# Layer 0's attention: turning the negated maxima on VectorE in squares of 32, and sixteen transfers a round into q's stacks

## The chip, the cores and the metric

The program runs on one core of one Trainium2 chip, as one launch. The time is the device time of one execution in microseconds (us). Three executions of the kernel before took 2251.18, 2256.95 and 2261.61 us; the median is 2256.95. A profile is one more execution, recorded by the hardware profiler.

A core has five engines that work side by side and wait for each other through semaphores: TensorE (PE in the profile; its weight loads are PEld), VectorE (DVE), ScalarE (ACT), GpSimd (POOL) and SyncE (SP), which here issues nearly all DMA transfers. Each engine takes its instructions in the order of the program.

## The reference, cut to what matters

The whole is a decoder of four layers on x of shape 4 x 512 x 128: each layer has a self-attention, a cross-attention and a feed-forward part. Only layer 0's self-attention is touched. It has 16 heads of 8 channels, a causal mask and a linear bias in the distance (ALiBi), and a temperature:

```python
att = jnp.einsum('bqhd,bkhd->bhqk', q, k) * scale
att = att / temperature
bias = slopes[:, None, None] * rel[None, :, :]
bias = jnp.where(causal[None, :, :], bias, -jnp.inf)
att = att + bias[None, :, :, :]
w = jax.nn.softmax(att, axis=-1)
y = jnp.einsum('bhqk,bkhd->bqhd', w, v).reshape(Bc, Tc, Cc)
return y @ W_proj + b_proj
```

The softmax is computed as exp(att - maximum over the keys), divided by its sum.

## The kernel before

**Stages.** `build` runs the parts one after another and weaves a main stream with a side chain: after each step of the main stream, a step of the side chain is emitted. In the first stage the main stream is `rounds` of `l0_attn`; the side chains are layer norms, the context of layer 0's cross-attention, that cross-attention for batches 0 and 1, and the router of the first feed-forward part. A planner then settles each engine's instruction order from the dependences and its own estimates of durations; within an engine that order is fixed when the program runs. The feed-forward part of layer 0 follows.

**Stacks.** For each group of four heads there is a stack `qs[g]` and a stack `ks[g]`: a tile of 99 rows, 4 heads and 512 tokens in bfloat16. A product of the two stacks sums over rows. Rows 0 to 71 hold q and k, each number split into three bfloat16 parts, rows 72 to 80 the position bias, and rows 96 to 98 of q's stack the three parts of the negated maximum of every query, against ones in k's stack. So the scores to find the maxima use 81 rows (line 1136), and the scores for `exp` use all 99 (line 1181): the maximum is then already subtracted in the product. That second product has keys on the partitions and queries along the free axis, so the negated maxima must lie along a row, while the reduction that makes them leaves queries on the partitions. They must be turned.

**Rounds.** An item is one batch with one group of four heads; there are 16 items. In round r the kernel works at once on the item `now` (scores and maxima, `score_units`, 11 units), on `prev` (the item before: its maxima are turned and its first 5 units of `exp` start) and on `old` (its last 6 units of `exp`, then `values`). Divisions and the closing product of a batch come for the item before that. A round has 11 steps; in each step one score unit and one unit of `exp` are emitted. The `exp` units of `old` fill steps 0 to 5, those of `prev` steps 6 to 10.

**The maxima.** At step 0 `shift` cuts the 128 x 16 negated maxima m (16 = 4 blocks of 128 tokens x 4 heads) into three bfloat16 parts with four small VectorE operations (lines 1155 to 1158; subtractions are recorded under the helper `tt`, line 436) and leaves them in `d3`. At step 2 `shift_rows` turns them: four TensorE transposes, one for each block of 128 tokens, into one PSUM bank of 12 x 512 (line 1165), one ScalarE copy to `d_rows` (line 1167), and four transfers from SyncE, one for each head, each of 3 rows of 512 tokens, into rows 96 to 98 of `qs[g]` (line 1169). At step 7 `load` issues six transfers (lines 1125 and 1126) that fill the stacks of the item two rounds on. In rounds 1, 5 and 9 (counted by the item whose maxima are turned), the projections of the next batch are computed and stored with four transfers (lines 1109 and 1111). All of these go through SyncE's one queue, in order.

Of the kernel before, what the change touches and what calls it, by code (L numbers as in the profile page):

```python
# [14 lines left out]
BF16 = mybir.dt.bfloat16  # L15
# [3 lines left out]
ALU = mybir.AluOpType  # L19
# [3 lines left out]
P = 128  # L23
B, S, D = 4, 512, 128
NT = B * S // P
TB = S // P
# [265 lines left out]
class Net:  # L292
# [745 lines left out]
    def l0_attn(self, pool, W, Wo):  # L1038
# [3 lines left out]
        nc, tc = self.nc, self.tc  # L1042
        one = lambda shape, name, dt=F32: pool.tile(shape, dt, name=name, bufs=1)
        K1, K2 = 81, 99
        qs = [one([K2, 4, S], f"qs{g}", BF16) for g in range(4)]
# [18 lines left out]
        rows = one([48, 16], "own_rows")  # L1064
# [8 lines left out]
        def biases():  # L1073
            ps = self.mm((1, D))
            self.dot(ps, *[(Wo["bv"][:, g : g + 1], Wo["wp"][:, g * D : g * D + D]) for g in range(4)])
            br = one([1, D], "br")
            self.tt(br, ps, Wo["bp"], ALU.add)
            wp0 = one([P, D], "wp0")
            nc.vector.tensor_copy(wp0, Wo["wp"][:, :D])
            nc.sync.dma_start(wp0[8:9, :], br)  # L1080
            wp.extend([wp0] + [Wo["wp"][:, g * D : g * D + D] for g in range(1, 4)])

        items = [(b, g) for b in range(B) for g in range(4)]
        made, ys, stacks = {}, {}, {}

        def project(b):

            xb = self.tokens(b)
            pq, pk = self.mm(), self.mm()
            self.dot(pq, (W["wq"], xb))  # L1090
            self.dot(pk, (W["wk"], xb))
            q, k = (pool.tile([P, S], F32, tag=n, name=n, bufs=1) for n in "qk")
            nc.vector.tensor_scalar(q, pq, W["bq"], sc, ALU.add, ALU.mult)
            nc.scalar.activation(k, pk, AF.Identity, bias=W["bk"])
            yield
            q3, k5 = pool.tile([P, 3, S], BF16, tag="q3", name="q3"), pool.tile([P, 5, S], BF16, tag="k5", name="k5")
            for a, out in ((q, q3), (k, k5)):
                nc.scalar.copy(out[:, 0], a)
                self.tt(a, a, out[:, 0], ALU.subtract)
            yield  # L1100
            for a, out in ((q, q3), (k, k5)):
                nc.scalar.copy(out[:, 1], a)
                self.tt(out[:, 2], a, out[:, 1], ALU.subtract)
            yield
            nc.gpsimd.tensor_copy(k5[:, 3:5], k5[:, 0:2])
            qd = self.away.tile([16, 24, S], BF16, name=f"q_parts{b}")
            kd = [self.away.tile([16, 24, S], BF16, name=f"k_parts{b}_{c}") for c in range(3)]
            flat = lambda d: d.rearrange("h (d p) t -> (h d) (p t)", p=3)
            nc.sync.dma_start(flat(qd), q3.rearrange("r p t -> r (p t)"))
            for c in range(3):  # L1110
                nc.sync.dma_start(flat(kd[c]), k5[:, c : c + 3].rearrange("r p t -> r (p t)"))
            stacks[b] = qd, kd
            yield
            ps = self.mm((P, TB, 16, 8))
            for j in range(TB):
                self.dot(ps[:, j].rearrange("p h d -> p (h d)"), (self.tile_of(TB * b + j), W["wv"]))
            nc.scalar.copy(vs[b % 2][:, :, :, :8], ps)
            yield

        def load(b, g):  # L1120

            qd, kd = stacks[b]
            for c in range(3):
                r = slice(24 * c, 24 * c + 24)
                nc.sync.dma_start(qs[g][r], qd[4 * g : 4 * g + 4].rearrange("h r t -> r h t"))
                nc.sync.dma_start(ks[g][r], kd[c][4 * g : 4 * g + 4].rearrange("h r t -> r h t"))

        def score_units(b, g):

            m = made[b, g, "m"] = pool.tile([P, TB, 4], F32, tag="m", name="m", bufs=2)  # L1130

            def unit(i, h0, per):
                n = (i + 1) * P
                ps = self.mm((P, per, n))
                for h in range(per):
                    nc.tensor.matmul(  # L1136
                        ps[:, h], lhsT=qs[g][:K1, h0 + h, i * P : n], rhs=ks[g][:K1, h0 + h, :n], start=h == 0, stop=False
                    )
                nc.tensor.matmul(  # L1139
                    ps[:, :, i * P :], lhsT=self.identb, rhs=self.causal.unsqueeze(1).to_broadcast([P, per, P]),  # L1140
                    start=False, stop=True,
                )
                nc.vector.tensor_reduce(m[:, i, h0 : h0 + per], ps, AX.X, ALU.max, negate=True)  # L1143

            return [
                lambda i=i, h0=h0, per=per: unit(i, h0, per)
                for i, per in ((3, 1), (2, 1), (1, 2), (0, 4)) for h0 in range(0, 4, per)
            ]

        def shift(b, g):  # L1150

            m = made.pop((b, g, "m"))
            d3 = made[b, g, "d"] = pool.tile([P, TB, 4, 3], BF16, tag="d3", name="d3")
            rest = pool.tile([P, TB, 4], F32, tag="d_rest", name="d_rest")
            nc.vector.tensor_copy(d3[..., 0], m)
            self.tt(rest, m, d3[..., 0], ALU.subtract)
            nc.vector.tensor_copy(d3[..., 1], rest)
            self.tt(d3[..., 2], rest, d3[..., 1], ALU.subtract)

        def shift_rows(b, g):  # L1160

            d3 = made.pop((b, g, "d"))
            t = self.bank("mm", [12, S], BF16)
            for i in range(TB):
                nc.tensor.transpose(t[:, i * P : i * P + P], d3[:, i].rearrange("q h p -> q (h p)"), self.identb)
            rows = pool.tile([12, S], BF16, tag="d_rows", name="d_rows", bufs=2)
            nc.scalar.copy(rows, t)
            for h in range(4):
                nc.sync.dma_start(qs[g][96:99, h, :], rows[3 * h : 3 * h + 3, :])

        def exp_units(b, g):

# [50 lines left out]
        def divide(b):  # L1223
            y = ys[b]
            dT = self.turned3(inv.pop(b), pool)
            for g in range(4):
                c = self.mm()
                self.dot(c, (pick[:, 4 * g : 4 * g + 4].rearrange("r h i -> r (h i)"), dT))
                self.tt(y[:, g, :], y[:, g, :], c, ALU.mult)
# [8 lines left out]
        def rounds(first, last):  # L1238
            n = len(items)
            item = lambda i: items[i] if 0 <= i < n else None  # L1240
            if first == 0:
                yield from project(0)
                load(0, 0)
                biases()
                load(0, 1)
                yield
            for r in range(first, last):
                now, prev, old, done = (item(r - i) for i in range(4))
                a = score_units(*now) if now else []
                if prev:  # L1250
                    made["units", prev] = exp_units(*prev)
                late = made.pop(("units", old))[5:] if old else []
                early = made["units", prev][:5] if prev else []
                ahead = project(now[0] + 1) if now and now[1] == 1 and now[0] + 1 < B else iter(())
                for i in range(11):
                    if i == 0 and prev:
                        shift(*prev)
                    if i == 2 and prev:
                        shift_rows(*prev)
                    if i < len(a):  # L1260
                        a[i]()
                    e = late[i : i + 1] if i < 6 else early[i - 6 : i - 5]
                    for unit in e:
                        unit()
                    yield
                    if i == 1 and done and done[1] == 3:
                        divide(done[0])
                        yield
                    if i == 4 and done and done[1] == 3:
                        close(done[0])  # L1270
                        yield
                    if i == 7 and old:
                        values(*old)
                        yield
                    if i == 9 and old and old[1] == 3:
                        sums(old[0])
                        yield
                    if i in (1, 3, 5, 8, 10):
                        next(ahead, None)
                    if i == 7 and item(r + 2):  # L1280
                        load(*item(r + 2))
# [1103 lines left out]
```

## Time and profile before

| what | value |
|---|---|
| time, median of 3 runs | 2256.95 us |
| the profiled execution's own time | 2272.79 us |
| its span, first to last instruction | 2271.0 us |
| mean granted TensorE clock | 0.957 |
| PE busy over the span | 2109.5 us, 93% |
| DVE busy over the span | 1608.1 us, 71% |
| ACT busy over the span | 995.4 us, 44% |
| attention stage, 40 to 253 us: PE busy | 196.05 us |
| the same: DVE busy | 153.62 us |
| the same: ACT busy | 127.92 us |
| d_rows transfers | 64 of 3.0 KB, first issue at 43.3 us, last at 253.1 us |

The span is divided among engines by busy time, and a chain of work is followed back from the last instruction. A busy share says how much an engine did, not what the end waited for; for that one reads, in the stage concerned, what each engine waited for and who released it. A row of the timeline has the start, the length, the engine, the line, the operation with output and inputs, the count, and in brackets the idle time before it and its releaser. A row of a line's list has shortest, median and longest duration in ns. A row of windows has the stretch, its length, the busy time of PE, PEld, DVE, ACT and POOL (instructions in brackets), then the granted TensorE clock as a share of full speed, the busy share of the DMA engines and GB/s. Lengths of matmuls are modelled and overlap.

### The profile page before, as it was taken

The page shows a single profiled execution, that of the slowest core. Times are in us where ns is not written, and L with a number is a line of the kernel's source. Part 1 is how long each engine was busy: PE and PEld are TensorE (multiplying, and loading weights), DVE is VectorE, ACT ScalarE, POOL GpSimd, SP SyncE. Part 2 cuts the span into 40 slices and gives each one's busy share as a digit, 9 for nine tenths or more (in the row PEclk, how much of TensorE's full clock was granted, in tenths as well). Part 3 has the DMA queues.
Part 4 walks back from the last instruction along what each step waited for, and adds up shares of the span by engine and source line. Part 5 has one row for each costly group of instructions (what it writes and reads, how often), then busy time and mean ns, then how long its engine had stood idle before and what let it go on. Part 6 is the DMA issues. An engine that isn't in the chain of part 4 may idle for free.

```text
span 2271.0 us, 28138 instructions
## 1 busy us (share of the span) xinstructions
PE 2109.5 (93%) x8946; PEld 1121.5 (49%) x8946; DVE 1608.1 (71%) x4059; ACT 995.4 (44%) x2042; POOL 554.8 (24%) x695
## 2 busy tenths in 40 slices
PE   6999899999999998999999999999999996697778
PEld 3566556544545553444444544444444443564463
DVE  6667576666675769787977797867777765886525
ACT  4556446444325452444434543443343434364421
POOL 1000001000000001433323343333333322336541
PEclk7989999999999999999999999999999998898869
DMA  6321134254453344334334444444443442200022
GB/s 167 99 65 44 45 111 123 62 137 112 112 143 84 105 101 107 75 100 110 110 83 105 114 120 114 124 111 107 114 114 101 111 129 46 94 1 6 20 54 76
DMA packets 88947, 213.26 MB, mean 94 GB/s; under 512 B 21874, under 2 KB 40626, under 8 KB 88542
## 3 DMA queue, kind: packets, MB, share of 16 engines
q1 hardware_dynamic: 85230, 207.52, 34.9%
q0 software_dynamic: 3568, 3.93, 0.6%
q8 instruction: 71, 1.16, 0.2%
q14 instruction: 78, 0.64, 0.1%
HBM read 182.33 MB, written 23.53 MB: 91 GB/s over the span
## 4 chain that ended last, share of the span: by engine, by line
PE 72%; DVE 15%; issue 5%; ACT 3%; POOL 2%; DMA 2%; SPq 1%; another core or an unknown queue 0%; POOLq 0%; DVEq 0%; ACTq 0%
PE mm L425 19%; PE f L425 13%; PE mm L1854 8%; PE s L425 8%; PE acc L1013 6%; PE mm L1826 4%; PE mm L1801 4%; DVE h L436 2%; PE mm L1136 1%; PE mm L1203 1%; PE mm L1181 1%; DVE at_m L1883 1%; DVE m L1143 1%; DVE gvx L436 1%; PE s L515 1%
## 5 line engine op out<-in xcount | busy, mean ns | idle before, releaser
L1762 POOL TENSOR_TENSOR gvx<-gvx 128x512 f32<-128x512 f32 (+1 forms) x256 | 260.3, 1017 | 549.3 <-DVE gvx L436 488.3
L425 PE MATMUL f<-xT,w_l_ffn 128*128 128x512 f32 (+1 forms) x768 | 369.3, 603 | 1.2 <-ACT h L1005 0.7
L1885 ACT ACTIVATE at_e<-mm,at_m 128x512 f32<-128x512 f32 x256 | 173.0, 685 | 293.1 <-DVE at_m L1883 274.3
L425 PE MATMUL mm<-w_l_ffn_qkv,xT 128*128 128x512 f32 x512 | 266.3, 604 | 4.2 <-ACT at_e L1885 1.7
L1854 PE MATMUL mm<-og,w_l_ffn_o 128*128 128x512 f32 x512 | 265.8, 603 | 3.2 <-DVE og L436 3.2
L436 DVE TENSOR_TENSOR h<-h,f 128x512 f32<-128x512 f32 (+1 forms) x192 | 131.1, 684 | 139.9 <-PE f L425 105.3
L1005 ACT ACTIVATE h<-f 128x512 f32<-128x512 f32 x189 | 112.3, 596 | 251.0 <-PE f L425 214.2
L425 PEld LDWEIGHTS f<-xT,w_l_ffn 128*128 128x128 f32 (+1 forms) x768 | 140.2, 192 | 151.0 <-issue 123.6
L1013 PE MATMUL acc<-h,w_l_ffn 128*128 128x512 f32 x378 | 194.8, 600 | 3.5 <-DVE h L436 2.9
L436 DVE TENSOR_TENSOR gvx<-mm,gv 128x512 f32<-128x512 f32 x256 | 174.5, 683 | 20.8 <-PE mm L425 17.1
L436 DVE TENSOR_TENSOR og<-mm,c 128x512 f32<-128x512 f32 x256 | 176.2, 690 | 18.3 <-PE mm L1854 16.0
L1802 ACT COPY eT<-mm 128x512 f32<-128x512 f32 x256 | 137.6, 596 | 83.4 <-PE mm L1801 83.2
L1883 DVE TENSOR_REDUCE at_m<-mm 128x1 f32<-128x512 f32 x256 | 161.1, 681 | 11.7 <-PE mm L425 10.3
L1801 PEld LDWEIGHTS mm<-ident,at_e 128*128 128x128 f32 x1024 | 120.2, 142 | 68.4 <-issue 47.7
L1854 PEld LDWEIGHTS mm<-og,w_l_ffn_o 128*128 128x128 f32 x512 | 91.7, 191 | 114.4 <-issue 90.3
L1801 PE MATMUL mm<-ident,at_e 128*128 128x128 f32 x1024 | 135.1, 274 | 5.3 <-ACT at_e L1885 5.3
L425 PEld LDWEIGHTS mm<-w_l_ffn_qkv,xT 128*128 128x128 f32 x512 | 87.3, 190 | 95.2 <-issue 59.0
L425 PE MATMUL mm<-roped 64*128 64x512 f32 x512 | 131.3, 622 | 1.7 <-DVE roped L436 1.0
L1143 DVE TENSOR_REDUCE m<-mm 128x1 f32<-128x512 f32 (+3 forms) x176 | 104.8, 635 | 32.6 <-PE mm L1139 31.7
L1826 PE MATMUL mm<-eT,v 128*64 128x512 f32 x512 | 118.7, 599 | 0.0
L1013 PEld LDWEIGHTS acc<-h,w_l_ffn 128*128 128x128 f32 x378 | 71.2, 192 | 93.1 <-issue 67.3
L436 DVE TENSOR_TENSOR h<-h,c 128x512 f32<-128x512 f32 x160 | 111.5, 703 | 4.1 <-DMA c<-l_ffn_w 1.3
(453 smaller groups left out, 3529.4 us busy)
## 6 DMA issues: line engine op xcount, KB each, us to landing
c<-gates SPq DMA_DIRECT2D x256, 256.0 KB
c<-l_ffn_w SPq DMA_DIRECT2D x96, 384.0 KB
w_l_ffn<-in_l_ffn SPq DMA_DIRECT2D x26, 576.0 KB
w_l_ffn_qkv<-in_l_ffn_qkv SPq DMA_DIRECT2D x16, 640.0 KB
w_l_ffn_o<-in_l_ffn_o SPq DMA_DIRECT2D x16, 512.0 KB
rot<-qk SPq DMA_DIRECT2D x128, 64.0 KB
d<-inverted SPq DMA_DIRECT2D x64, 128.0 KB
k_parts<-k SPq DMA_DIRECT2D x12, 384.0 KB
```

The lines of the kernel that those rows point to most:

```text
L425: self.nc.tensor.matmul(out, lhsT=lhsT, rhs=rhs, start=i == 0, stop=i == len(pairs) - 1)
L436: self.nc.vector.tensor_tensor(out, a, b, op)
L1005: nc.scalar.activation(h, pg, AF.Silu)
L1013: nc.tensor.matmul(acc["t"], lhsT=W["d" + u], rhs=h, start=i == 0, stop=i == n - 1)
L1143: nc.vector.tensor_reduce(m[:, i, h0 : h0 + per], ps, AX.X, ALU.max, negate=True)
L1762: nc.gpsimd.tensor_tensor(x[:, :, :m], x[:, :, :m], x[:, :, m : 2 * m], ALU.add)
L1801: nc.tensor.transpose(p[:, j, :], es[i][hl][:, j * P : j * P + P], self.ident)
L1802: nc.scalar.copy(eT[hl][:, :, i * P : i * P + P], p)
L1826: nc.tensor.matmul(po[64 * hl : 64 * hl + 64, :], lhsT=m["v"][:, j, hl, :], rhs=eT[hl][:, j, :], start=j == 0, stop=j == TB - 1,)
L1854: nc.tensor.matmul(acc, lhsT=W["o"][:, (e - 1) * D : e * D], rhs=hs.pop(e - 1), start=e == 1, stop=e == E)
L1883: nc.vector.tensor_reduce(m, s, AX.X, ALU.max, negate=True)
L1885: nc.scalar.activation(e[:, :n], s, AF.Exp, bias=m, accum_out=den)
```

## The change

`d3` becomes one tile that stays, 128 x 4 x 32 in bfloat16, cleared once on GpSimd. Of each 32 columns the first 12 hold the parts (4 heads x 3 parts). `shift` writes them there with the same four small operations, and then turns the whole tile on VectorE with one instruction, which turns each square of 32 partitions x 32 columns in itself. After it, partition 32k + 3h + p holds, for block j and the 32 columns of that square, part p of head h for the tokens 128j + 32k to 128j + 32k + 31. The four groups of 32 partitions therefore hold different tokens, and each head's row is put together by four transfers: 4 groups x 4 heads make sixteen a round, each of 3 rows and 4 runs of 32 tokens (64 bytes). They are issued group by group, with the heads inside. `shift_rows`, with its transposes, its PSUM bank and its ScalarE copy, is gone, and so is its call at step 2.

```diff
+        d3 = one([P, TB, 32], "d3", BF16)
+        nc.gpsimd.memset(d3, 0.0)
+
         def shift(b, g):
 
             m = made.pop((b, g, "m"))
-            d3 = made[b, g, "d"] = pool.tile([P, TB, 4, 3], BF16, tag="d3", name="d3")
+            parts = d3[:, :, :12].rearrange("q j (h p) -> q j h p", p=3)
             rest = pool.tile([P, TB, 4], F32, tag="d_rest", name="d_rest")
-            nc.vector.tensor_copy(d3[..., 0], m)
-            self.tt(rest, m, d3[..., 0], ALU.subtract)
-            nc.vector.tensor_copy(d3[..., 1], rest)
-            self.tt(d3[..., 2], rest, d3[..., 1], ALU.subtract)
-
-        def shift_rows(b, g):
-
-            d3 = made.pop((b, g, "d"))
-            t = self.bank("mm", [12, S], BF16)
-            for i in range(TB):
-                nc.tensor.transpose(t[:, i * P : i * P + P], d3[:, i].rearrange("q h p -> q (h p)"), self.identb)
-            rows = pool.tile([12, S], BF16, tag="d_rows", name="d_rows", bufs=2)
-            nc.scalar.copy(rows, t)
-            for h in range(4):
-                nc.sync.dma_start(qs[g][96:99, h, :], rows[3 * h : 3 * h + 3, :])
+            nc.vector.tensor_copy(parts[..., 0], m)
+            self.tt(rest, m, parts[..., 0], ALU.subtract)
+            nc.vector.tensor_copy(parts[..., 1], rest)
+            self.tt(parts[..., 2], rest, parts[..., 1], ALU.subtract)
+            rows = pool.tile([P, TB, 32], BF16, tag="d_rows", name="d_rows", bufs=2)
+            nc.vector.transpose(rows.rearrange("q j r -> q (j r)"), d3.rearrange("q j r -> q (j r)"))
+            for k in range(4):
+                for h in range(4):
+                    nc.sync.dma_start(
+                        qs[g][96:99, h, :].rearrange("p (j k r) -> k p j r", k=4, r=32)[k],
+                        rows[32 * k + 3 * h : 32 * k + 3 * h + 3],
+                    )
...
                     if i == 0 and prev:
                         shift(*prev)
-                    if i == 2 and prev:
-                        shift_rows(*prev)
```

## The prediction

> **What bounds the kernel now.** I read the page first (busy shares, chain), then the attention stage alone, 40 to 253 us.
>
> ```profile
> span 2271.0 us, 28138 instructions
> PE 2109.5 (93%) x8946; PEld 1121.5 (49%) x8946; DVE 1608.1 (71%) x4059; ACT 995.4 (44%) x2042; POOL 554.8 (24%) x695
> PE 72%; DVE 15%; issue 5%; ACT 3%; POOL 2%; DMA 2%; SPq 1%; another core or an unknown queue 0%; POOLq 0%; DVEq 0%; ACTq 0%
> ```
>
> TensorE is the bound nearly everywhere, and runs in order: a wait at its head that nothing fills lengthens the run. In this stage it is busy 196.05 of 213 us, so it has about 17 us to give. The whole change lies here, in a loop: the maxima of round r-1 are cut into three parts, turned, and carried by DMA into rows 96 to 98 of q's stack, which the first `exp` unit of round r (line 1181, 99 rows) reads. Round 3 in the timeline of all engines (start us, length us):
>
> ```profile
> 63.50 0.68 DVE L1143 TENSOR_REDUCE m<-mm 128x1 f32<-128x512 f32 x1
> 64.52 0.18 DVE L436 TENSOR_TENSOR d<-d_rest,d 128x16 bf16<-128x16 f32 x1
> 64.75 0.39 PE L1165 MATMUL mm<-identb,d 128*12 128x128 bf16 x4 [1.35 <-DVE d L436]
> 65.22 0.57 ACT L1167 COPY d_rows<-mm 12x512 bf16<-12x512 bf16 x1 [1.29 <-PE mm L1165]
> 65.83 2.78 SPq L1169 DMA_DIRECT2D qs<-d_rows  x4
> 67.64 0.38 PE L1181 MATMUL mm<-qs,ks 99*128 99x512 bf16 x1
> 68.33 0.10 PEld L1181 LDWEIGHTS <-ks 99*128 99x128 bf16 x1 [0.31 <-DMA qs<-d_rows]
> 74.08 0.17 DVE L1155 CAST d<-m 128x16 bf16<-128x16 f32 x1
> ```
>
> The reader is to see that there is no slack left. The first transfer is issued at 65.83 and head 0's matmul starts at 67.64: 1.8 us from issue to use. Head 1's transfer starts about 0.7 us later and head 1's matmul, at 68.33, is released by it. The list of line 1169 gives what one such issue holds SyncE for, and one 512-byte transfer in sixteen pieces of 32 bytes (line 1080) shows that pieces do not raise it:
>
> ```profile
> L1169 SPq DMA_DIRECT2D qs<-d_rows x64: 639/642/782, 43.3 to 253.1; - x64
> L1080 SPq DMA_DIRECT2D wp<-br x1: 638/638/638, 25.3 to 25.3; - x1
> ```
>
> Four take 2.78 us: 0.64 plus a gap of 0.07, 0.71 us from one to the next.
>
> **What goes.** Sixteen rounds each lose four PE transposes (0.39 us), one ScalarE copy (0.57) and TensorE's wait for d (1.35 in round 3). The path from the last small VectorE operation to SyncE, 64.70 to 65.83, 1.1 us, goes with them.
>
> **What comes.** One VectorE turn of 128x128 bf16. The trace has no such operation: from the 0.17 us of a 128x16 cast to the 0.68 us of a 128x512 reduction; the Trainium skill ("VectorE: DVE Perf Modes", The three transpose paths) states 311 ns, between the two. I take 0.3. The memset on POOL comes once, before the rounds, off the path. Then sixteen issues on SyncE in place of four. Head 0 reads all 512 tokens, and the transfers go block by block with the heads inside, so head 0 is complete with the thirteenth: 12 x 0.71 = 8.5 us after the first issue. Landing of the thirteenth: 1.8 us as now (3 rows either way; four runs of 64 bytes each instead of one of 1024; from 1.5 to 2.3).
>
> **What is moved.** In the changed program's instruction order the turn does not follow the four small operations at once. In eight of the rounds (3, 4, 7, 8, 11, 12, 13, 15) score reductions of the running round stand between them: cast, reduction, subtraction, reduction, cast, reduction, subtraction, reduction, turn. Reductions run 0.57 apart in this stage (0.6 with the switch), the small ones 0.2: 4 x 0.6 + 3 x 0.2 + 0.3 + 0.1 = 3.4 us from the first cast to SyncE. Before, round 3 needed 65.83 - 63.43 = 2.4.
>
> So from the first cast to head 0's matmul: 3.4 + 8.5 + 1.8 = 13.7 us. Before, from the timeline, in those eight rounds: 4.21, 4.22, 4.80, 5.17, 4.85, 5.17, 4.26, 4.63, in all 37.3. Increase: 8 x 13.7 - 37.3 = 72.3 us. The others, by how many operations stand before the turn:
> - Rounds 1 and 16 (none): 1.1 + 8.5 + 1.8 = 11.4, before 5.23 and 4.57: +6.2 and +6.8.
> - Round 2 (one reduction): 12.0, before 5.96: +6.0.
> - Rounds 5 and 9 (a reduction and q's scaling, 0.8): 12.8, before 5.28 and 5.69: +7.5 and +7.1.
> - Rounds 6, 10 and 14: TensorE has the closing products of a batch in that stretch, 11.1, 16.1 and 13.2 us; the transfers need about 12.5: +1.5, 0, 0. These products are the cover.
>
> Sum +107 us. From head 0's matmul to the next round's cast is TensorE's own stream, 6.4 us in plain rounds (67.64 to 74.08), and passes on unchanged: heads 1 to 3 arrive 0.71 apart, no faster than TensorE takes them. The next round waits for this stretch, so nothing absorbs the delay; the planner only moves work of the side chain (layer norm, cross-attention of batches 0 and 1, the router) ahead of head 0 in rounds 7, 8, 11, 12 and 13. That takes some 2 us from elsewhere and fills, but does not shorten, the wait: +105.
>
> What queues behind the sixteen on SyncE: six loads of q's and k's stacks for two rounds on (0.41 each), and in three rounds q's and k's stores. 16 x 0.71 + 6 x 0.41 = 13.8 us a round against a new round of 13.7 + 6.4 = 20 us: SyncE doesn't become a bound of its own, and the loads have a round to spare.
>
> **The clock.** TensorE would now stand some 8 to 10 us in thirteen rounds (it reaches head 0 about 4 us after the cast). What idling does to it shows after round 1 and at the stage's end (windows; the third number from the right is the granted clock):
>
> ```profile
> 43.00:46.00 3.00, 1.45 (x12) 0.69 (x10) 3.00 (x6) 2.62 (x6) 0.00 (x0) 1.00 0.01 2
> 46.00:50.00 4.00, 2.94 (x17) 1.58 (x17) 4.00 (x7) 2.13 (x4) 1.04 (x1) 0.62 0.52 125
> 50.00:54.00 4.00, 4.00 (x19) 2.87 (x17) 2.43 (x8) 1.62 (x4) 0.00 (x0) 0.53 1.01 356
> ...
> 265.00:268.00 3.00, 0.76 (x6) 0.52 (x6) 1.40 (x5) 0.57 (x1) 0.00 (x0) 0.57 0.58 152
> 268.00:272.00 4.00, 3.95 (x13) 2.54 (x13) 2.48 (x4) 1.29 (x2) 0.00 (x0) 0.50 1.04 249
> 272.00:275.00 3.00, 3.00 (x16) 3.00 (x16) 0.00 (x0) 0.00 (x0) 0.00 (x0) 0.50 1.01 223
> ```
>
> After some 3 us of idling at 265 the clock stays at half for about 7.5 us of full work. The Trainium skill ("TensorE: Matmul & The Clock Gate", Part 1) says the same in a rule that speaks against this change: an idle window of about 3.4 us halves the clock, a busy one restores it, and the windows run free. By row and rule half speed lasts 3.4 to 7.5 us after each long wait and costs half of that, 1.7 to 3.7 us; I take 2.8. Thirteen rounds give 36 us, less about 8 for half-clock spells that the stage already has (the one at 46 to 54, which the new wait swallows, and part of the others): +28. Without the gate the sum would stay at +105.
>
> A second rule says the opposite of my main term: "DMA: Bandwidth & Descriptors", Issuing engines are not separate DMA queues, calls the issuing time usually small beside the transfer. Here the row decides: 0.64 us of issue against 1.8 us to use, for 3 KB in all. Were it small, say 0.05, head 0 would wait 3.4 + 0.6 + 1.8 = 5.8 us and the eight rounds would lose only 8 x 5.8 - 37.3 = 9 us together.
>
> **Sum.** 105 + 28 = +133 us. The profiled execution took 2272.79 us (span 2271.0); with 133 it is 2406. The median of the runs shown, 2256.95, lies 16 below that execution; the same difference gives 2390.
>
> **Rivals.**
> 1. Issue-bound, clock free: the wait as above, but what follows it is held by VectorE (reductions 0.57 apart) and ScalarE (`exp` 0.56) so that a halved TensorE costs little. Against: the values matmuls, 2.3 us a round, are TensorE alone. +105: 2362.
> 2. Pieces cost: twelve runs of 64 bytes raise the issue to about 1.0 us or slow three DMA engines. Against: line 1080's row. 12 x 1.0 + 5.2 = 17.2 us, 3.5 more in thirteen rounds, with the clock +180: 2437.
> 3. Issues are cheaper: q's loads, also 3-D but from DRAM, take 0.37. Then 12 x 0.41 = 4.9, the wait 10.1, 3.6 less in thirteen rounds: +60 to +85, about 2330.
> 4. Faster: the issue overlaps fully and head 0 is released by the first-landed transfers. It decides where the spacing falls below some 0.05 us and VectorE, no longer held up by TensorE's stop at the transposes, turns a reduction or two sooner, so that the path is under the 4.7 us of before; then the PE transposes, their waits (up to 1.35 us in six rounds) and the copies are gain, 5 to 15 us: 2245. Against: 0.71 is measured for the same source, destination and row count.
> 5. The change does nothing: the wait is filled by the side chain. Against: that chain has about 10 us in all, against 105.
>
> **How the numbers follow.** Forecast 0.70; rivals 1 to 5: 0.11, 0.09, 0.06, 0.03, 0.01. The forecast's own spread (landing 1.5 to 2.3, half clock 1.7 to 3.7) is about 2370 to 2420. Range 2345 to 2440: it takes in rival 1 and the lower half of rival 2, and leaves out rivals 3 to 5 and the upper half of 2, some 15 in 100. A measurement of this kernel tells about 0.5% (11 us) from no change: faster 0.03, same 0.01, slower 0.96.
>
> **What would show it.** In the profile after: line 1167's issue near 640 ns, sixteen in some 11.3 us per round; TensorE's weight loads before the 99-row matmuls waiting for d_rows for 80 to 120 us in all (7.2 before); 13 to 14 us from the first cast to head 0 in rounds 3 and 4; granted clock about half in the stage's windows after each wait; the stage's end some 130 us later and all after it alike. Wrong would be: an issue far from 0.64, a release before the thirteenth transfer, or a clock that stays full.

## The result, and the profile after

The changed kernel takes 2390.79 us (median; 2388.53 to 2392.19) against 2259.28 us (2251.18 to 2264.16) for the kernel before: 1.0579 times as long, 95% interval 1.0551 to 1.0606, or 131.5 us more. The forecast was 2390, range 2345 to 2440.

The page's head (span, busy time of each engine) of the kernel after:

```profile
span 2389.7 us, 28258 instructions
PE 2128.1 (89%) x8882; PEld 1120.6 (47%) x8882; DVE 1615.5 (68%) x4075; ACT 989.8 (41%) x2026; POOL 554.8 (23%) x696
```

TensorE has 64 instructions fewer (the transposes), ScalarE 16 fewer (the copies), VectorE 16 more (the turns), POOL one more (the memset). TensorE's share falls from 93% to 89%: the added time is time in which it stands. Where that is, three stretches of the run show (length of the stretch, busy PE, PEld, DVE, ACT, POOL, granted clock, DMA share, GB/s). Before, from the end of the attention stage on:

```profile
253.00:2173.00 1920.00, 1811.22 (x6929) 938.55 (x6928) 1386.66 (x3429) 832.16 (x1721) 504.26 (x630) 0.97 0.38 98
2173.00:2271.00 98.00, 78.69 (x288) 45.01 (x286) 43.08 (x83) 21.58 (x47) 31.24 (x32) 0.85 0.14 46
```

After, the attention stage, and then the same two stretches:

```profile
40.00:391.00 351.00, 221.11 (x1596) 130.75 (x1593) 161.46 (x452) 122.32 (x232) 11.40 (x12) 0.75 0.14 40
391.00:2311.10 1920.10, 1813.27 (x6927) 938.75 (x6927) 1386.49 (x3429) 831.92 (x1720) 503.81 (x630) 0.97 0.38 98
2311.10:2389.70 78.60, 69.88 (x288) 38.10 (x286) 42.66 (x83) 21.72 (x47) 31.19 (x32) 0.98 0.18 58
```

The middle, 1920 us, is the same to 0.1 us. The attention stage is 138 us longer (head 0 of round 16 starts at 390.56 instead of 252.79). The last stretch is 19 us *shorter* after, with the same instructions at a clock of 0.98 instead of 0.85. That is a property of the one execution that was profiled before, which the prediction found 16 us above the median: in the traces of all nine other kernels of this document, from their last 288 matmuls on, this stretch takes 78.9 to 79.4 us, in the trace of before 98.5. So the spans differ by 118.7, the medians by 131.5, and the stage by 138. The reader should take the stage from the traces and the total from the medians. The 6.5 us between these two lie within the spread of the kernel before (2249.37 to 2267.90 us in 27 executions) and are not explained further.

Round 3 in the timeline of the kernel after (start, length, engine, line, operation, and in brackets the idle time before it and its releaser), to set beside round 3 of before:

```profile
79.88 0.18 DVE L1159 CAST d<-m 128x16 bf16<-128x16 f32 x1
...
82.46 0.31 DVE L1164 STREAM_TRANSPOSE d_rows<-d 128x128 bf16<-128x128 bf16 x1
82.80 12.01 SPq L1167 DMA_DIRECT2D qs<-d_rows  x16
93.69 0.58 PE L1182 MATMUL mm<-qs,ks 99*128 99x512 bf16 x1 [11.28 <-DMA qs<-d_rows]
...
102.74 0.18 DVE L1159 CAST d<-m 128x16 bf16<-128x16 f32 x1
```

From the cast to the first issue 2.9 us, sixteen issues in 12.0 us (0.75 us apart), and head 0's matmul 10.9 us after the first issue. Twelve spacings are 9.0 us, so the thirteenth transfer leaves at 91.8 and is used 1.9 us later. TensorE stood for 11.28 us just before. The list of line 1167 (shortest, median, longest ns) has the new transfers; the turn, line 1164, is listed with 295, 306 and 314 ns, sixteen times:

```profile
L1167 SPq DMA_DIRECT2D qs<-d_rows x256: 702/703/886, 41.7 to 391.1; - x128
```

TensorE's waits in the attention stage (total, times, longest; matmuls, then weight loads), after and then before:

```profile
PE mm L1182 <- DMA qs<-d_rows: 112.1, 13, 11.5
PEld L1182 <- DMA qs<-d_rows: 75.9, 19, 11.8
```

```profile
PE mm L1181 <- DMA qs<-d_rows: 1.8, 2, 1.5
PEld L1181 <- DMA qs<-d_rows: 7.2, 15, 1.8
```

And the granted clock (third number from the right) over round 3, after and then before:

```profile
82.00:86.00 4.00, 0.41 (x3) 0.10 (x1) 1.67 (x5) 0.76 (x2) 0.00 (x0) 0.99 0.10 25
86.00:90.00 4.00, 0.00 (x0) 0.00 (x0) 0.00 (x0) 0.00 (x0) 0.00 (x0) 0.50 0.01 1
94.00:98.00 4.00, 4.00 (x22) 1.30 (x24) 0.56 (x1) 1.19 (x2) 0.00 (x0) 0.50 0.38 104
98.00:102.00 4.00, 4.00 (x40) 2.24 (x33) 1.76 (x3) 1.96 (x4) 0.00 (x0) 0.80 0.58 167
```

```profile
60.00:74.00 14.00, 12.62 (x127) 7.38 (x119) 9.41 (x19) 9.84 (x18) 0.00 (x0) 1.00 0.44 116
```

From 86 to 90 no engine computes, and the DMA engines are idle too (0.01): only SyncE issues. When TensorE starts again it is fully busy, but at half clock for the first 4 us and more.

To compare kernels, each round is split at two events that all of them have: the first cast of the maxima, and head 0's 99-row matmul. The sums, in us, over the stage (cast to head 0: 16 rounds; head 0 to the next cast: 15), with the time for which TensorE's clock was at half between 36 and 420 us (read in windows of 1 us):

| kernel | cast to head 0 | head 0 to next cast | sum | half clock | median, us | ratio (95%) |
|---|---|---|---|---|---|---|
| before | 104.4 | 108.4 | 212.8 | 54 | 2256.96 to 2259.92 | 1 |
| after | 216.4 | 133.8 | 350.2 | 192 | 2390.79 | 1.0579 (1.0551 to 1.0606) |
| heads_outer | 132.9 | 179.6 | 312.5 | 148 | 2371.42 | 1.0473 (1.0422 to 1.0525) |
| pe_turn_16 | 214.1 | 133.4 | 347.5 | 167 | 2392.78 | 1.0575 (1.0532 to 1.0619) |
| clock_kept | 217.1 | 114.0 | 331.1 | 47 | 2378.73 | 1.0529 (1.0482 to 1.0576) |
| two_queues | 167.1 | 130.0 | 297.1 | 145 | 2347.89 | 1.0386 (1.0352 to 1.0419) |
| turn_8 | 129.5 | 129.4 | 258.9 | 96 | 2305.78 | 1.0200 (1.0167 to 1.0232) |
| turn_4 | 103.2 | 118.4 | 221.6 | 71 | 2267.71 | 1.0042 (1.0027 to 1.0058) |

The ratios of the last six are against the kernel before on the same chip, which had a median of 2256.96 beside heads_outer, pe_turn_16, clock_kept and turn_4, and of 2259.92 beside the others.

### The profile page after: what moved, and what is told of

It reads as the page before. It is cut to its first block, busy times and chain, and to the rows that moved or that the text cites. A ratio compares the mean times of both kernels' runs of the same rounds, so it can differ in the third digit from the quotient of the medians.

```text
span 2389.7 us, 28258 instructions
## 1 busy us (share of the span) xinstructions
PE 2128.1 (89%) x8882; PEld 1120.6 (47%) x8882; DVE 1615.5 (68%) x4075; ACT 989.8 (41%) x2026; POOL 554.8 (23%) x696
## 5 line engine op out<-in xcount | busy, mean ns | idle before, releaser
L1182 PE MATMUL mm<-qs,ks 99*128 99x512 bf16 (+3 forms) x256 | 71.6, 335 | 114.4 <-DMA qs<-d_rows 112.1
L1882 DVE TENSOR_REDUCE at_m<-mm 128x1 f32<-128x512 f32 x256 | 161.2, 683 | 10.6 <-PE mm L425 9.2
L1190 ACT ACTIVATE e<-mm 128x512 f32<-128x512 f32 (+1 forms) x176 | 94.0, 563 | 154.6 <-PE mm L1186 150.8
L1825 PE MATMUL mm<-eT,v 128*64 128x512 f32 x512 | 118.7, 599 | 0.0
```

The source lines that it names most:

```text
L1825: nc.tensor.matmul(po[64 * hl : 64 * hl + 64, :], lhsT=m["v"][:, j, hl, :], rhs=eT[hl][:, j, :], start=j == 0, stop=j == TB - 1,)
L1882: nc.vector.tensor_reduce(m, s, AX.X, ALU.max, negate=True)
```

## The experiments

**The theory**: the sixteen issues on one sequencer hold head 0 until the thirteenth, and TensorE then runs on at half clock; the turn itself costs nothing. **Its rivals**: the VectorE turn, or its place among the reductions, costs; a head is released only when the whole set has landed; the spacing is set by the transfers and not by the sequencer; the clock costs nothing.

**heads_outer**: the two loops swapped, so that a head is complete with every fourth transfer.

```diff
-            for k in range(4):
-                for h in range(4):
+            for h in range(4):
+                for k in range(4):
```

> The changed kernel with its two loops swapped: all four transfers of head 0 first, then those of head 1, and so on. Theory (SyncE's issue, 0.75 us from one to the next, sets the wait; a head is released by its own four transfers): head 0 starts after the fourth, at 2.9 + 3 x 0.75 + 1.85 = 7.0 us from the first cast, head 3 after the sixteenth, at 16.0 us, and 2.1 us later comes the next cast: 18.1 us a round against 20.2, and the one long stop becomes four stops of under 3 us, so that the clock should stay high for most of it. In 13 rounds 27 us from the order and up to 28 from the clock: 2336 to 2364 us. Rival (the head waits for the whole set of sixteen, or for the turn): no change, 2390.

Measured 2371.42 us, above the forecast's upper end. Round 3 of this kernel's timeline:

```profile
79.27 11.98 SPq L1167 DMA_DIRECT2D qs<-d_rows  x16
83.52 0.58 PE L1182 MATMUL mm<-qs,ks 99*128 99x512 bf16 x1 [4.62 <-DMA qs<-d_rows]
86.41 0.58 PE L1182 MATMUL mm<-qs,ks 99*128 99x512 bf16 x1 [1.77 <-DMA qs<-d_rows]
```

Head 0 starts 4.25 us after the first issue, as three spacings of 0.75 and a landing of 2 make it, and head 1 comes 2.9 us behind it. So a head is released by its own four transfers, and the rival of the whole set falls. From cast to head 0 it is 83.5 us shorter than after over the stage. But heads 1 to 3 now arrive four issues apart, and the stretch after head 0 grows by 45.8: the stage's sum is 37.7 us less than after's. The miss has two parts. The clock hardly recovers: 148 us at half. The forecast had four stops of under 3 us and a clock that stays high. In round 3 the stop ahead of head 0 is still 4.6 us, and in round 1, where the stops are 2.8, 1.8, 1.7 and 2.1 us with work between them, the clock is at half from 46.0 to 59.6. A window of that stretch of heads_outer:

```profile
50.00:54.00 4.00, 1.48 (x6) 0.55 (x5) 1.39 (x2) 0.74 (x2) 0.00 (x0) 0.50 0.02 3
```

So several short stops close together kept the clock down as a long one does. And part of the gain is given back later: the lead over the kernel after is 34 us when the first feed-forward activation starts, 24 us when `gvx` is first computed (1018.0 against 1042.4), 20 us at the end. The last of these steps is not this kernel's own: from the first `gvx` on GpSimd to the last stretch, five of the ten traces take 1266.5 to 1267.7 us (the kernel after among them) and the other five 1271.4 to 1271.9. The first step back, from that activation on, in windows of the kernel after and then of heads_outer (columns as above):

```profile
416.50:500.30 83.80, 82.65 (x297) 43.16 (x297) 58.26 (x212) 39.89 (x74) 8.10 (x11) 1.00 0.44 123
```

```profile
382.40:472.00 89.60, 86.01 (x297) 44.81 (x297) 58.36 (x212) 39.90 (x74) 8.12 (x11) 0.96 0.42 114
```

The same 297 matmuls take 5.8 us longer. TensorE's clock is 0.96 instead of 1.00 (its busy time is 3.4 us longer), and one 2.7 us wait for a transfer of weights (`w_s`) stands in it that the kernel after does not have. The stretch after it, to the first `gvx`, loses 3.9 us more at a clock of 0.98 instead of 0.99. Why the clock differs there is open.

**pe_turn_16**: the kernel before, with its transposes and its ScalarE copy, but sixteen transfers (each of 3 rows and one run of 128 tokens) in place of four. The edit against the kernel before:

```diff
-            for h in range(4):
-                nc.sync.dma_start(qs[g][96:99, h, :], rows[3 * h : 3 * h + 3, :])
+            for i in range(TB):
+                for h in range(4):
+                    nc.sync.dma_start(qs[g][96:99, h, i * P : i * P + P], rows[3 * h : 3 * h + 3, i * P : i * P + P])
```

> The kernel before, with TensorE's transposes and ScalarE's copy, but sixteen transfers a round: each head's row goes in four transfers of 3 rows x 128 tokens, block by block with the heads inside. Theory (the number of issues is the cost): head 0 comes 2.4 + 12 x 0.75 + 1.85 = 13.2 us after the first cast, nearly as in the changed kernel: 2375 to 2395 us. Rival (the VectorE turn and its late place, or the 64-byte runs, cost the time): at most 30 us above the kernel before, 2260 to 2290.

Measured 2392.78 us: the same as the kernel after, with the old turn. Round 3 of its timeline:

```profile
81.69 10.97 SPq L1170 DMA_DIRECT2D qs<-d_rows  x16
91.70 0.59 PE L1182 MATMUL mm<-qs,ks 99*128 99x512 bf16 x1 [8.04 <-DMA qs<-d_rows]
```

Sixteen transfers in place of four, and nothing else changed, bring the whole loss: it does not need the VectorE turn. Here sixteen issues take 10.97 us (median 640 ns each) where the pieces of 64 bytes take 12.01 (703): the four runs a row cost 0.06 us each issue. In round 3 that makes head 0 come 10.0 us after the first issue instead of 10.9; over the stage the two kernels differ by only 2.7 us.

**clock_kept**: the changed kernel with 34 to 46 matmuls of the turned tile with a tile of ones, in eleven rounds, ahead of the first `exp` unit. Their product is used by nothing; they only keep TensorE busy while it would wait.

```diff
+        wide = one([P, S], "wide", BF16)
+        nc.gpsimd.memset(wide, 1.0)
+        busy = {1: 34, 2: 36, 3: 46, 4: 46, 5: 36, 8: 46, 9: 36, 12: 34, 13: 34, 15: 46, 16: 44}
+
+        def occupy(n):
+            rows = made["rows"].rearrange("q j r -> q (j r)")
+            for i in range(n):
+                if i % 16 == 0:
+                    ps = self.mm()
+                nc.tensor.matmul(ps, lhsT=rows, rhs=wide, start=True, stop=True)
...
-            rows = pool.tile([P, TB, 32], BF16, tag="d_rows", name="d_rows", bufs=2)
+            rows = made["rows"] = pool.tile([P, TB, 32], BF16, tag="d_rows", name="d_rows", bufs=2)
...
+                    if i == 6 and prev:
+                        occupy(busy.get(r, 0))
```

> The changed kernel with TensorE kept busy in its long stops: 34 to 46 matmuls of 128x512 whose result nobody reads stand ahead of the first exp unit in rounds 1 to 5, 8, 9, 12, 13, 15 and 16 (rounds 7 and 11, filled by the side chain, are left alone). They depend on the turn and are sized to end before the transfers land. Theory (half clock after each stop costs some 28 us): eleven of thirteen rounds keep the clock near 1.0, 20 to 30 us are saved: 2360 to 2372 us. Rival (clock free: VectorE and ScalarE hold the stretch after the stop): 2385 to 2395. If the fill overruns, each round shows it as a matmul of the fill running when the transfers have landed.

Measured 2378.73 us (2372.21 to 2386.66), above the forecast's upper end of 2372. Round 3 of its timeline:

```profile
81.10 12.01 SPq L1177 DMA_DIRECT2D qs<-d_rows  x16
81.13 10.10 PE L1161 MATMUL mm<-wide,d_rows 128*128 128x512 bf16 x46 [0.41 <-ACT e L1200]
91.92 0.39 PE L1192 MATMUL mm<-qs,ks 99*128 99x512 bf16 x1 [0.68 <-DMA qs<-d_rows]
98.47 0.18 DVE L1169 CAST d<-m 128x16 bf16<-128x16 f32 x1
```

The wait for the data is as long as in the kernel after (10.8 us from the first issue to head 0; 217.1 us from cast to head 0 in all), so the fill doesn't lengthen it. But head 0's matmul takes 0.39 us instead of 0.58, and the next cast comes 6.55 us after it instead of 9.05: 6.4 was the kernel before's. Over the stage that is 19.8 us (133.8 to 114.0), with 47 us at half clock instead of 192. So the half clock costs, and the rival that says otherwise falls. The medians differ by only 12 us. All four executions are below the lowest of the kernel after (2388.53), but the profiled one is the fastest of them: in the order of their times, 2372.21, 2376.24, 2381.22 and 2386.66, their mean granted clocks fall, 0.964, 0.960, 0.958 and 0.954. So 19.8 us is what the fill gives back where it works best.

**turn_4**: the VectorE turn, with before's four transfers of 3 rows of 512 tokens. It leaves out the gathering: three quarters of each row are zeros, and part of the rest belongs to other tokens. It shows what the turn would cost if four transfers were enough.

```diff
+        turns = [one([P, S], f"turns{i}", BF16) for i in range(2)]
+        for t in turns:
+            nc.gpsimd.memset(t, 0.0)
...
-            rows = pool.tile([P, TB, 32], BF16, tag="d_rows", name="d_rows", bufs=2)
-            nc.vector.transpose(rows.rearrange("q j r -> q (j r)"), d3.rearrange("q j r -> q (j r)"))
-            for k in range(4):
-                for h in range(4):
-                    nc.sync.dma_start(
-                        qs[g][96:99, h, :].rearrange("p (j k r) -> k p j r", k=4, r=32)[k],
-                        rows[32 * k + 3 * h : 32 * k + 3 * h + 3],
-                    )
+            rows = turns[(4 * b + g) % 2]
+            nc.vector.transpose(rows[:, : TB * 32], d3.rearrange("q j r -> q (j r)"))
+            for h in range(4):
+                nc.sync.dma_start(qs[g][96:99, h, :], rows[3 * h : 3 * h + 3])
```

> The changed kernel with the turn on VectorE but only four transfers a round, one for each head, of 3 rows x 512 tokens from a tile whose columns past 128 stay zero. Most queries get no shift and some a wrong one, so the softmax's numbers differ; the amount of work is that of a kernel with four transfers. Theory (only the number of issues costs): first cast to head 0 takes 2.9 + 1.85 = 4.8 us, as before on average (4.7), TensorE's stops at the transposes are gone: 2245 to 2262 us, and the clock as before. Rival (the turn or its place behind reductions costs): 2270 or more.

Measured 2267.71 us over 20 runs, 1.0042 (1.0027 to 1.0058): between the two expectations. Round 3 of its timeline:

```profile
66.52 2.77 SPq L1169 DMA_DIRECT2D qs<-turns  x4
68.34 0.39 PE L1181 MATMUL mm<-qs,ks 99*128 99x512 bf16 x1 [2.20 <-DMA qs<-turns]
```

Cast to head 0 takes 4.73 us in this round (4.21 before) and 103.2 us in all (104.4): what leaves with the transposes and the copy comes back as the reductions that stand between the cast and the turn. The stretch after head 0 is 10 us longer over the stage, in rounds 1, 7, 11, 13 and 15, by 1.4 to 2.6 us each. In the last four of these, 7.9 us together, the clock is at half for 3.1 to 5.5 us; before, it was at full there. In round 1 the planner's order of the side chain differs. Even if the turned parts could go in four transfers, this turn would gain nothing here.

**turn_8**: as turn_4, with eight transfers of 256 tokens, so that head 0 is complete with the fifth.

```diff
...
-            for k in range(4):
+            for k in range(2):
                 for h in range(4):
                     nc.sync.dma_start(
-                        qs[g][96:99, h, :].rearrange("p (j k r) -> k p j r", k=4, r=32)[k],
-                        rows[32 * k + 3 * h : 32 * k + 3 * h + 3],
+                        qs[g][96:99, h, 256 * k : 256 * k + 256], rows[32 * k + 3 * h : 32 * k + 3 * h + 3, :256]
                     )
```

> The changed kernel with eight transfers a round, two for each head, of 3 rows x 256 tokens; half of the tokens get the wrong shift (their numbers are those of other squares), the work is otherwise the same. Theory: head 0 comes with the fifth transfer, 2.9 + 4 x 0.75 + 1.85 = 7.8 us after the first cast, 3.1 more than before in 13 rounds: +40 without the clock; [...]+40 to +65: 2297 to 2325. Rival (a threshold, not a slope): 2257 or 2390.

Measured 2305.78 us, within the theory's expectation. Round 3 of its timeline:

```profile
70.75 5.53 SPq L1170 DMA_DIRECT2D qs<-turns  x8
75.37 0.59 PE L1184 MATMUL mm<-qs,ks 99*128 99x512 bf16 x1 [5.00 <-DMA qs<-turns]
```

4.6 us from issue to head 0, four spacings of 0.70 and the landing. Four, eight and sixteen transfers give 2267.71, 2305.78 and 2390.79 us: 9.5 and then 10.6 us for each transfer added to a round. So it is a slope: had there been slack for some added issues, the step from four to eight would have been the cheaper one by far.

**two_queues**: the issues of every second group of partitions from ScalarE's queue.

```diff
-                    nc.sync.dma_start(
+                    (nc.scalar if k % 2 else nc.sync).dma_start(
```

> The changed kernel with the transfers of two of the four partition groups issued by ScalarE instead of SyncE, eight each. Theory (the issuing sequencer sets the spacing): head 0 comes with the seventh of each queue, 2.9 + 6 x 0.75 + 1.85 = 9.3 us after the first cast against 13.8; 4.5 us in 13 rounds is 58, less what ScalarE's exp units lose by standing behind 8 issues: 2315 to 2345 us. Rival (the DMA engines or their descriptor generation set the spacing, whoever issues): 2380 to 2395.

Measured 2347.89 us, 3 us above the expected range. Round 3 of its timeline:

```profile
81.87 6.31 SPq L1167 DMA_DIRECT2D qs<-d_rows  x8
81.87 6.16 ACTq L1167 DMA_DIRECT2D qs<-d_rows  x8
87.16 0.58 PE L1182 MATMUL mm<-qs,ks 99*128 99x512 bf16 x1 [5.67 <-DMA qs<-d_rows]
```

Two sequencers issue two sets of eight at once, 0.80 and 0.78 us apart instead of 0.75, and head 0 comes after 5.3 us instead of 10.9. So the sequencer sets the spacing, not the transfers. The gain is smaller in rounds 2, 7 and 11 (cast to head 0 of 10.7 to 12.4 us against 8.2 in rounds 3 and 4), and in rounds 1 and 10 there is none (12.7 and 20.5 us against after's 12.2 and 13.4). In rounds 1, 2 and 10 the two engines do not issue together: SyncE starts its eight 4.1 to 6.2 us after ScalarE. In rounds 7, 10 and 11 ScalarE work of the side chain or of the batch's division stands behind the eight issues in ScalarE's order, and TensorE waits 6.4 to 7.2 us for its result.

**exp_later_3 and exp_later_2**: the kernel before, with the `exp` units one step later, to see whether the rest of its wait for the transposes is worth anything; the transposes at step 3 in the first, at step 2 in the second.

```diff
-                late = made.pop(("units", old))[5:] if old else []
-                early = made["units", prev][:5] if prev else []
+                late = made.pop(("units", old))[4:] if old else []
+                early = made["units", prev][:4] if prev else []
...
-                    e = late[i : i + 1] if i < 6 else early[i - 6 : i - 5]
+                    e = late[i : i + 1] if i < 7 else early[i - 7 : i - 6]
```

> The kernel before with the exp units of a round one step later (four of eleven in their own round, seven in the next) and the transposes at step 3 instead of 2. It asks whether the loop cast, turn, transfer, head 0 already bound the kernel before: its tight rounds have TensorE waits of 1.35 us at the transposes and 0.3 at the first exp unit. Theory (it did, at the edge): up to 1.5 us in eight rounds, 2243 to 2255 us. Rival (other engines take up the room): 2257 within 0.5%.

> As exp_later_3, with the transposes left at step 2. Theory: TensorE still stops at the transposes for 1.35 us in tight rounds, only the waits at the first exp unit go (7 us in all in weight loads): 2250 to 2257. Rival: no change.

Measured 2262.03 us (1.0005; 0.9987 to 1.0022) and 2259.31 us (1.0002; 0.9985 to 1.0018): no change in either. The traces show the gain in the plain rounds and its loss elsewhere: from one first cast to the next, round 3 takes 10.43 and 10.40 us instead of 10.65, but rounds 6, 7 and 14 are longer in both, and the stage's sums are 217.7 and 213.4 us against 212.8. No version tried beats the kernel before.

## Why the prediction was right

It was right in time and in cause. That the median fell within 1 us of the forecast is luck: some terms were off and offset each other. The stage grew by 138 us instead of 133, and the medians by 131.5.

- **Issue**: predicted 0.64 us and 0.71 apart, measured 0.703 and 0.75. "Pieces do not raise it", read from line 1080, was slightly wrong, since that row is of another form than four runs in each of three rows: 12 spacings are 9.0 us instead of 8.5. Rival 2's reason was thus right in sign, at a sixth of its size (0.06 for 0.36).
- **Landing**: 1.8 taken, 1.9 measured. **Release by the thirteenth transfer**: as predicted; heads_outer moves it to the fourth.
- **First cast to SyncE**: 3.4 predicted for the eight interleaved rounds, 2.9 measured in round 3. There a pair of a reduction and a small operation takes 0.68 us (reductions start at 79.95, 80.64, 81.31 and 81.99), not 0.8. The turn, 0.3 by the price in the Trainium skill ("VectorE: DVE Perf Modes", The three transpose paths: 311 ns), is 0.306 here.
- **Cast to head 0**: 13.7 us predicted in those eight rounds, 111.6 / 8 = 13.95 measured. In all rounds +112.0 against +107 (+105 with the side chain). The closing products of rounds 6, 10 and 14 were named as the cover: +2.7, -2.7 and -0.4 against +1.5, 0 and 0, so they are.
- **Clock**: +28 predicted, and the stretch after head 0 grew by 25.4. The thirteen rounds in which it has half clock grew by 1.9 us on average, rounds 6 and 14, in which it has none, by 0.1 and 0.4. So the number per stop was mis-sized (2.8 taken, less 8 in all for spells that were there already), and the total nearly right. clock_kept takes back 19.8; its own stretches after head 0 still have 24 us at half (after 72, before 11). An estimate from these: 25.4 us for 61 us of added half clock make 5.4 us for the 13 us that it has more than before, and that is the 5.6 us that it does not take back.
- **The rule of the clock**: the Trainium skill ("TensorE: Matmul & The Clock Gate", Part 1) agrees with the windows of round 3: the clock is 0.99 from 82 to 86, half by 86, some 3.5 us after TensorE stopped at 82.4, half through the rest of the stop and 5.9 us beyond it. For short stops the traces decide otherwise than its idle window of 3.4 us. In the stage of the ten traces, the clock was at half no later than 1 us after every stop of TensorE (no matmul and no weight load) of 4 us or more. But so it was after 27 of the 37 stops of 2 to 4 us that began at full clock: after one of 2.28 us in turn_8, for instance, and not after one of 2.19 us in turn_4.
- **The row at 265** was misread: "some 3 us of idling" did not come first. TensorE stood from 265.13 to 266.76, 1.6 us, and the clock was at half from 265.4 to 275.6. Ahead of it, from 261.3, TensorE had only 32 small matmuls (128x4), which the trace records as busy. What brought the clock down there is open. The row gave the upper end of the time at half clock, 7.5 us; after the kernel after's stops of 8 us and more it is 3.5 to 6.4. The waits at the transposes, "up to 1.35 us", have one of 1.9, which changes nothing in the sum.
- **The rule that was set aside**: the Trainium skill ("DMA: Bandwidth & Descriptors", Issuing engines are not separate DMA queues) calls issuing time usually small beside the transfer. Here sixteen issues are 12.0 us beside a landing of 1.9, and by pe_turn_16 they are the whole loss.
- **The step from 2406 to 2390**, carrying over the 16 us between the profiled execution and the median, held: those us lay in the last stretch of that one execution, as the second window line of before shows beside the nine other traces. The prediction gave no reason for it.
- **Rivals**: 1 (clock free) falls by clock_kept; 3 (cheaper issue) by line 1167; 4 (faster) by the slope of turn_8 and turn_4; 5 by the stage. Of 4, the gain that was to be had without the spacing, 5 to 15 us, isn't there: turn_4, which has no added spacing, is some 10 us slower instead.

## What to carry to other kernels

Count the transfers that stand between a producer and the first instruction that uses them, multiply by the issue spacing in the trace, and add it to the path. A cheaper turn on another engine is worth nothing if it leaves its result in more pieces: here each added transfer cost about 10 us over sixteen rounds. Where a wait makes TensorE stand for 4 us or more, add about 2 us for the half clock that followed each such stop here; shorter stops, and several in a row, brought it down too, though not each of them.

## What was not expected of the hardware

- An issue of 3 rows from SyncE takes 640 to 642 ns (medians) for one run of 256, 512 or 1024 bytes a row, but 703 ns for four runs of 64 bytes, and 734 ns if ScalarE issues these. Side by side, SyncE and ScalarE issue every 0.80 and 0.78 us, SyncE alone every 0.75.
- A small VectorE operation between two reductions adds only 0.07 us to their spacing (0.67 instead of 0.60, medians after), though it is listed with 0.17 to 0.19.
- Nearly all spells at half clock in the ten traces last 3.4 us or a multiple of it: those of before that the prediction shows, 46.94 to 53.77 and 265.40 to 275.64, are two and three times that long.
- The same last stretch of the program took 98.0 us in one execution and 78.6 in another, at clocks of 0.85 and 0.98: a span from one profile carries such a difference, and only a comparison by stage finds it.
